# Layer 2's dense product by seven block products, with its sums in the last attention step, and another order of VectorE's work

## The chip, the cores and the metric

The kernel runs on one core of a Trainium2 chip. The time is the device time of one execution in microseconds (us). Nine executions of the kernel before lie between 1560.4 and 1579.48 us, with a median of 1569.6. One more was profiled. The names of the engines in the profile are PE (TensorE), PEld (its weight loads), DVE (VectorE), ACT (ScalarE), POOL (GpSimd) and SP (SyncE, which here issues DMAs only).

## The reference: four layers on 1024 tokens

The input `x` holds 8 sequences of 128 tokens with 512 features, in float32. Four layers add to it in turn, `x = x + ffn(cond(x))`. Layers 0, 1 and 3 are gated low-rank layers. Layer 2, which the change touches, is grouped attention over a paged cache followed by a dense layer with a small mixture:

```
q = rope(rmsnorm(x Wq));  k = rope(rmsnorm(x Wk));  v = x Wv        # 32 query heads, 8 key heads, D = 128
scores = q [k_cache[block_table], k]^T / sqrt(D), masked beyond cache_seqlens
o = softmax(scores) [v_cache[block_table], v];   y = o Wo             # y: 1024 x 512

H = y W^T + b                                                         # the dense product, 1024 x 512 x 512
z = y A                                                               # rank 32
w = weights of 8 experts, from H[anchor tokens, :8] and (z LiMEs^T)[anchor tokens]
x = x + H + ((z * (w LiMEs)) Bmat) * scaling
```

`w` needs only eight columns of H on every second token, and these are computed apart from H.

## The kernel before, in words

**Layout.** Tokens lie in 8 blocks of 128. `x` stays in SBUF turned: features on partitions, [128, 4 chunks, 1024 tokens]. Layer 2's attention output `y` is built with tokens on partitions, and each block is transposed by TensorE into `y2T`, which is laid out as `x` is.

**Attention.** `run` (line 1275) goes over 16 steps: 8 head groups (`qd`), and in each 4 pairs of blocks (`p`). Step `n` does the scores and exponentials of its first block (`weigh(n, 0)`, line 1122), the sums of the exponentials over the five key chunks (`added`, line 1144), the division and output block sums of the step before (`divided`, `outputs`), the projection of the step after (`project(n + 1)`, line 1000), the rotary terms (`rotate`, line 1041), the output projection of the step before (`leave(n - 1)`, line 1201), and then the second block's scores mixed with the first block's value products (`mix`, line 1176), the softmax sums by matmul (`summed`), their reciprocals (`inverted`) and the second block's value products. `project` and `leave` do a 2x2 block product with seven block products instead of eight (`seven`, line 952, Strassen's scheme in Winograd's form): sums of the blocks are made on VectorE beforehand, and partial results are added on VectorE between products that stay in the same PSUM banks. Their argument `at` names the places in `seven` where other engines' work is put into the order: "one", "six", "u1", "u2", "c22", "c11", "c12".

Keys and rotated queries are turned by VectorE in 32x32 squares into a buffer "kt", written to DRAM by four DMAs (`turn_cached`, line 1086, for the cached keys; `turn`, line 1102, for the new ones) and read back in the turned form (`fetch`, line 1113). Both use the one "kt" buffer. `gather` (line 899) reads cached keys and values by indirect DMAs that POOL issues.

**What sets the order.** Every instruction that goes through `kept` (line 855) is pinned behind the one traced before it on its engine. What does not go through it is placed by the framework's planner, which simulates the program. Before the change the functions of `ending` (line 1690) that deal with layer 2's dense part are mostly not pinned, and neither are the two loads of its weights.

**Layer 2's dense part.** `load_w2` and `load_aw` (lines 1748, 1752) load W and layer 3's A at step 14, into the buffers of the attention weights. `shifted` (line 1785) adds the bias to `x` with two POOL instructions of 128x2048. `turn` (line 1756) transposes a block of `y`; `low` and `anchors` (lines 1764, 1773) compute z and the routing columns from it, for blocks 0 to 3 at the end of step 14 and for 4 to 7 after the last step. `product(b)` (line 1792) does 16 matmuls of 128x128 by 128 columns for one block into a PSUM bank that stays open; `delta` (line 1879) adds the low-rank part into the same bank and VectorE adds the bank to `x` (line 1888, 128x512). `layer2` (line 2141) calls these, with `routing` (a chain of some twenty small VectorE instructions, line 1806) and `gains` (line 1855), and then prepares layer 3's weights on TensorE (`weights_turned`, `fold_scores`).

**Layer 3** already has a class `Seven` (line 1975) for block products of 256 columns: `begin` does the first product and copies it, `go_on` does the other six with three additions on VectorE between them. An open result is spread over two PSUM banks and two SBUF tiles; `last` (line 2124) adds these to `x`.

Of the kernel before, what the change touches and what calls it, by code (L numbers as in the profile page):

```python
# [17 lines left out]
P = 128  # L18
# [29 lines left out]
def forward(ctx: ExitStack, tc: tile.TileContext, a: dict, out: bass.AP):  # L48
# [615 lines left out]
    with psa:  # L664
# [73 lines left out]
        end.layer2(y2, bank, do=range(NB - 2, NB))  # L738
# [22 lines left out]
    with tc.If(redo > 0):  # L761
        sp.dma_start(x, kept)
        y2 = attention_any(tc, a, x, ident, lens, kvrow, part, ww, wop, ypool, eps, rows, chunks, mm)
        with ExitStack() as c3:
# [19 lines left out]
            end.layer2(y2, bank)  # L784
# [3 lines left out]
def attention(tc, a, x, ident, lens, kvrow, part, ww, wop, ypool, sums, rot, eps, psa, c2, chunks, mm):  # L788
# [412 lines left out]
    def leave(n, at={}):  # L1201
# [10 lines left out]

        def to_last(u):
            kept(pool.tensor_tensor(y(1, 1), u, y(1, 1), ALU.add))

        def to_middle(u):
            t = y2[:, 2 * p : 2 * p + 2, :].rearrange("p j d -> p (j d)")[:, HW : 3 * HW]
            t = t.rearrange("p (k d) -> p k d", k=2)
            kept(pool.tensor_tensor(t, t, u.unsqueeze(1).to_broadcast([P, 2, HW]), ALU.add))  # L1219
# [55 lines left out]
    def run(pool_, end_of, bank, keep):  # L1275
# [11 lines left out]
        rotate(1)()  # L1287
# [11 lines left out]
        for n, (qd, p) in enumerate(steps):  # L1299

            after = n + 1 if 0 < n < len(steps) - 1 else None
            weigh(n, 0)
            sums_of, outs = added(n, 0), iter(())
            next(sums_of)
            some(w_ops)()
            if n:
                divided(n - 1)
                outs = outputs(n - 1)
            every(sums_of)
            if after:  # L1310
# [7 lines left out]
                if n + 2 < len(steps):  # L1318
# [7 lines left out]
                    "u2": lambda: (keys_terms(), every(wo_ops)),  # L1326
                    "c22": lambda: (rotated(after), normed(after), turn(after)),
# [3 lines left out]
            elif n:  # L1331
                every(outs)
                leave(n - 1)
            else:
                read_cached = turn_cached(1)
                every(tokens(2))
                gather(2, "k")
            if n + 2 == len(steps):
                end.load_w2()
                end.load_aw()  # L1340
                end.shifted()
            mixed = mix(n, 0)
            weigh(n, 1, {2: (some(mixed),), 3: (some(mixed),), 4: (some(mixed, NC),)})
            if n == 0:
                fetch(1, read_cached)
            every(added(n, 1))
# [4 lines left out]
            inverted(n)  # L1351
            if n == 5:
                prepared = end.prepare(bank, lambda shape, name: wk.tile(shape, F32, tag="xs", name=name, bufs=1))
# [22 lines left out]
        end.product(0, "st", bank)  # L1376
        leave(n)
        return y2, end
# [311 lines left out]
def ending(  # L1690
# [25 lines left out]


    L3 = SimpleNamespace()
    Y2T = []
# [27 lines left out]

    def load_w2():
        W["2"] = tile_of_w2([P, DC, D], "WT2")
        sp.dma_start(W["2"], chunks(a["W2T"]))  # L1750

    def load_aw():
        W["a"] = tile_of_aw([P, DC, D], "AwT")
        sp.dma_start(W["a"], chunks(a["AwT"]))
# [30 lines left out]
    def shifted():  # L1785

        for g in range(TG):
            pool.tensor_tensor(
                x[:, :, half(g)], x[:, :, half(g)], bcol.unsqueeze(2).to_broadcast([P, DC, 512]), ALU.add
            )  # L1790

    def product(b, tag, bank):

        ps = bank(tag, [P, DC, P], f"h_{b}")
        for o in range(DC):
            for c in range(DC):
                mmq(
                    ps[:, o, :], W["2"][:, c, o * P : (o + 1) * P], Y2T[0][:, c, b * P : (b + 1) * P],
                    o == 0 and c == 0, False,
                )  # L1800
        H[b] = ps
# [77 lines left out]
    def delta(g):  # L1879

        zp, Bm = Z["zp"], L3.Bm
        for o in range(DC):
            for j in range(HB):
                mmq(H[g * HB + j][:, o, :], Bm[slot(j), o * P : (o + 1) * P], zp[slot(j), g, :], False, True)
        for j in range(HB):
            b = g * HB + j
            t = x[:, :, b * P : (b + 1) * P]
            dve.tensor_tensor(t, H[b], t, ALU.add)
# [60 lines left out]

    def left_sums(a11, a12, a21, a22, t, by):
        s1, s2, s3, s4 = (t[:, k] for k in range(4))
        for o, l, r, op in (
            (s1, a21, a22, ALU.add), (s2, s1, a11, ALU.subtract),
            (s3, a11, a21, ALU.subtract), (s4, a12, s2, ALU.subtract),
        ):
            by.tensor_tensor(o, l, r, op)
        return a11, a12, a22, s1, s2, s3, s4

    def right_sums(b11, b12, b21, b22, t):
        t1, t2, t3, t4 = (t[:, k] for k in range(4))
        for o, l, r in ((t1, b12, b11), (t2, b22, t1), (t3, b22, b12), (t4, b21, t2)):
            dve.tensor_tensor(o, l, r, ALU.subtract)
        return b11, b21, b22, t1, t2, t3, t4

    def left(t, k):

        return [t[:, 2 * j : 2 * j + 2, (2 * k + i) * P : (2 * k + i + 1) * P] for i in range(2) for j in range(2)]

    def right(t, g):

        return [t[:, 2 * i : 2 * i + 2, g * 512 + j * 256 : g * 512 + (j + 1) * 256] for i in range(2) for j in range(2)]

    class Seven:


        def __init__(self, name, bank, A, B):
            self.A, self.B = A, B
            self.even, self.odd = (bank("mm", [P, 2, 256], f"{name}_{i}") for i in range(2))  # L1980
            self.p1, self.u = (
                L3.w3.tile([P, 256], F32, tag=f"seven_{n}", name=f"{n}_{name}", bufs=2) for n in ("p", "u")
            )
            self.c = {(0, 0): (self.even[:, 0], None), (0, 1): (self.odd[:, 1], self.u),
# [288 lines left out]
```

## Time and profile before

| | |
|---|---|
| median of 9 executions | 1569.6 us |
| lowest, highest | 1560.4, 1579.48 us |
| the profiled execution | 1572.14 us |
| its span in the profile | 1570.3 us |
| mean granted TensorE clock | 0.993 |
| DMA | 169.92 MB, mean 108 GB/s |

By the timeline of TensorE the attention steps run from 332 to 1426 us, about 34 us for most of them. The end of layer 2, from the last value products to layer 3's first matmul, is the stretch from 1414 to 1470 us; layer 3 ends the program.

In a line of the timeline the first number is the start in us from the span's beginning, then the length, the engine, the line of the kernel, the operation, output and inputs, the shape, and the number of instructions in the row. Brackets hold the engine's idle time just before and what ended it. One float32 matmul is two MATMUL instructions here. A line of the waits gives engine, tile and line of the waiting instruction, what released it, the sum in us, how many times, and the longest. A line of the windows gives start and end of a stretch, its length, the busy time (and instructions) of PE, PEld, DVE, ACT and POOL, the granted clock, the DMA engines' busy share, and GB/s.

### The profile page before, as it was taken

The numbers are of one execution on the slowest core, as the hardware profiler recorded it, in microseconds if no ns is written. First come the engines' busy times: TensorE is split into PE (matmuls) and PEld (weight loads), VectorE is DVE, ScalarE is ACT, GpSimd is POOL, SyncE is SP. The second block draws the span as 40 slices with busy tenths as digits, with TensorE's granted clock in tenths as the row PEclk, the third lists the DMA queues.
The fourth block names the chain that finished last, engine by engine and source line by source line (L and its number), as shares of the span: only waits on it lengthen the run. The fifth ranks groups of instructions, "written<-read, shape, count | busy, mean of one in ns | idle before, by whom it ended". The sixth has DMA issues, their size and how long they took to land.

```text
span 1570.3 us, 19040 instructions
## 1 busy us (share of the span) xinstructions
PE 1523.2 (97%) x6127; PEld 952.5 (61%) x6127; DVE 1063.0 (68%) x2055; ACT 540.1 (34%) x1332; POOL 861.0 (55%) x874
## 2 busy tenths in 40 slices
PE   9999999989999999999999999999999999999998
PEld 7878786535555555555555555655555555558887
DVE  4666434477877777777777677777777878744375
ACT  1111110144444444444443434544444444310110
POOL 1331105285766777767677766767766777622220
PEclk9999999999999999999999999999999999999999
DMA  9111002144654444553454444345454435512001
GB/s 300 41 41 31 1 0 62 52 137 104 176 149 132 143 121 129 145 155 98 126 163 118 123 139 146 99 131 170 119 138 119 138 98 147 145 41 90 1 2 56
DMA packets 157837, 169.92 MB, mean 108 GB/s; under 512 B 54272, under 2 KB 129216, under 8 KB 157600
## 3 DMA queue, kind: packets, MB, share of 16 engines
q1 hardware_dynamic: 139296, 131.27, 29.8%
q0 software_dynamic: 17056, 36.49, 8.0%
q8 instruction: 51, 0.84, 0.2%
q10 hardware_dynamic: 1376, 0.85, 0.2%
q14 instruction: 58, 0.48, 0.1%
HBM read 113.89 MB, written 42.07 MB: 99 GB/s over the span
## 4 chain that ended last, share of the span: by engine, by line
PE 85%; DVE 8%; DMA 3%; issue 2%; POOL 1%; SPq 1%; ACT 0%; ACTq 0%; DVEq 0%; POOLq 0%
PE av L1181 17%; PE st L1130 17%; PE g L362 7%; PE q_six L966 7%; PE wo_two L966 5%; PE dn L362 5%; PE q_five L966 4%; PE q_one L966 4%; PE wo_six L966 3%; PE wo_one L966 3%; PE eo_l L53 2%; PE h L1710 2%; DVE os L925 2%; PE z L1710 2%; PE midp_l L53 1%
## 5 line engine op out<-in xcount | busy, mean ns | idle before, releaser
L909 POOL DMA_INDIRECT kn<-in_k_cache,kvrow_k x256 | 285.9, 1117 | 73.2 <-issue 69.2
L1181 PE MATMUL av<-pT,vals 128*128 128x512 f32 x640 | 300.4, 600 | 0.0
L909 POOL DMA_INDIRECT vals<-in_v_cache,kvrow_v x256 | 259.1, 1012 | 73.4 <-issue 62.9
L1134 ACT ACTIVATE pT<-st,hide 128x512 f32<-128x512 f32 x256 | 175.9, 687 | 333.7 <-PE st L1130 203.7
L1130 PE MATMUL st<-qT,kT 128*128 128x512 f32 x512 | 238.3, 598 | 1.7 <-DMA qT<-turned_new 1.7
L1055 POOL TENSOR_TENSOR vq<-q,txq 128x256 f32<-128x256 f32 x128 | 120.4, 967 | 185.7 <-DVE q L1015 110.0
L1181 PEld LDWEIGHTS av<-pT,vals 128*128 128x128 f32 x640 | 119.6, 191 | 145.0 <-issue 142.7
L1130 PEld LDWEIGHTS st<-qT,kT 128*128 128x128 f32 x512 | 98.0, 192 | 111.5 <-issue 108.4
L1150 DVE TENSOR_TENSOR part<-pT 128x512 f32<-128x512 f32 x128 | 88.3, 692 | 71.8 <-issue 44.0
L1166 DVE RECIPROCAL rr<-sum 128x256 f32<-128x256 f32 x32 | 56.2, 1757 | 58.2 <-PE sum L1159 50.7
L966 PE MATMUL q_one<-q,x 128*128 128x384 f32 x256 | 93.0, 486 | 0.0
L1039 ACT ACTIVATE sqq<-q 128x128 f32<-128x128 f32 x256 | 79.4, 310 | 25.7 <-DVE q L1015 18.8
L966 PEld LDWEIGHTS q_one<-q,x 128*128 128x128 f32 x256 | 48.5, 190 | 39.8 <-issue 14.4
L966 PE MATMUL q_six<-q_s,xs_all 128*128 128x384 f32 x192 | 69.8, 486 | 0.0
L1219 POOL TENSOR_TENSOR y<-y,uo 128x512 f32<-128x512 f32 x32 | 41.3, 1291 | 48.0 <-DVE y L1211 47.5
L966 PE MATMUL wo_one<-o,oT 128*128 128x256 f32 x256 | 65.7, 379 | 0.0
L1130 PE MATMUL st<-qT,kTn 128*128 128x512 f32 x128 | 65.4, 592 | 0.0
L1020 ACT COPY q<-q_one 128x256 f32<-128x256 f32 x32 | 11.9, 372 | 149.6 <-PE q_one L966 149.6
L966 PE MATMUL wo_two<-o_s,os 128*128 128x256 f32 x256 | 60.6, 380 | 2.4 <-DVE os L925 2.2
L966 PE MATMUL q_six<-q_s,x 128*128 128x384 f32 x128 | 48.9, 504 | 10.3 <-DVE vals L1015 10.3
L429 POOL TENSOR_TENSOR ws<-wu 128x256 f32<-128x256 f32 (+1 forms) x9 | 6.8, 756 | 94.2 <-DMA wu<-in_WuT 94.2
L1134 ACT ACTIVATE pT<-st,rs 128x512 f32<-128x512 f32 x64 | 44.0, 687 | 38.4 <-PE av L1181 19.6
(448 smaller groups left out, 2840.5 us busy)
## 6 DMA issues: line engine op xcount, KB each, us to landing
turned_new<-qkt SPq DMA_DIRECT2D x126, 160.0 KB
turned_cached<-kt SPq DMA_DIRECT2D x128, 128.0 KB
kT<-turned_cached SPq DMA_DIRECT2D x32, 512.0 KB
qT<-turned_new SPq DMA_DIRECT2D x32, 512.0 KB
R<-R SPq DMA_DIRECT2D x96, 128.0 KB
q<-in_WqT SPq DMA_DIRECT2D x8, 1024.0 KB
o<-in_WoT SPq DMA_DIRECT2D x8, 1024.0 KB
kn<-in_k_cache,kvrow_k POOLq DMA_INDIRECT x256
```

The source lines that it names most:

```text
L53: pe.matmul(o, lhsT, rhs, start=start, stop=stop)
L362: pe.matmul(o, lhsT, rhs, start=start, stop=stop, skip_group_check=True)
L909: kept(pool.indirect_dma_start(out=d[:, c, :], out_offset=None, in_=kc if what == "k" else vc, in_offset=bass.IndirectOffsetOnAxis(ap=kvro ...
L966: kept(pe.matmul(o, l[:, c, :], r[:, c, :], start=start and c == 0, stop=c == 1, skip_group_check=True))
L1039: kept(act.activation(sq, S[n][m][:, j, i, :], AF.Square, accum_out=S[n]["ssq"][:, j, col : col + 1]))
L1055: kept(pool.tensor_tensor(to, t[:, b, :, hi : hi + 64], wx[:, b, lo : lo + 64].unsqueeze(2).to_broadcast(list(to.shape)), ALU.mult,))
L1130: kept(pe.matmul(ps, s["kT"][:, c, 4 * j : 4 * j + 4, :] if c < 4 else s["kn"][:, j], s["qT"][:, :, REP * j : REP * (j + 1), :].rearrange( ...
L1134: kept(act.activation(pT[:, c, :, :].rearrange("p i t -> p (i t)"), ps, AF.Exp, **(dict(bias=hide[:, b, c : c + 1]) if c < 4 else dict(bia ...
L1150: kept(dve.tensor_tensor(o, l, r, ALU.add))
L1166: kept(dve.reciprocal(r, S[n]["sum"]))
L1181: kept(pe.matmul(ps, v[:, c, :], pT[:, c, :, :].rearrange("p i t -> p (i t)"), start=c == 0, stop=c == NC - 1, skip_group_check=True,))
L1710: return pe.matmul(o, lhsT, rhs, start=start, stop=stop, skip_group_check=True)
```

## The change

1. The dense product is done by four `Seven`s (two halves of the tokens `g`, two halves of the output features `k`) instead of eight calls of `product`: 56 matmuls of 256 columns for 128 of 128 columns. `Seven` is split in `begin`, `go_on` (three products) and `end` (three more), and `into_x` adds its results to `x`: three additions of an SBUF tile and four of a PSUM block, each 128x256, on VectorE.
2. `delta` gets banks of its own, and still adds 128x512 from each to `x`.
3. The block sums of W (eight VectorE instructions of 128x256, `product_weights`) and those of the first half of `y2T` (four of 128x512, `product_tokens(0)`) are placed in step 15 behind the first block's scores and ahead of `added(15, 0)`. Those of the second half come in `layer2`.
4. The `begin` and `go_on` of the first half come before `leave(15)`, the `end`s behind it: one before the last transposes, the other behind `low(1)` and `anchors(1)`, all pinned.
5. In step 15 `outputs(14)` goes ahead of the remaining sums of `added`, and `leave(14)` moves into the second block's scores, behind the third of them.
6. `leave(15)` has its last two additions on VectorE instead of POOL.
7. In `leave`'s "c22" slot the addition of the finished block now goes ahead of the weight sums and of the key's straight terms, which stood in "u2" ahead of it.
8. At the beginning `turn_cached(1)` moves from step 0 to before `turn(1)`; in step 0 `fetch(1)` and `gather(2, "k")` move behind the first two part sums of the second block, and `tokens(2)` behind the reciprocal.
9. `shifted` becomes four ACT instructions of 128x1024, in step 15 behind its last exponential; before, the planner placed its two POOL instructions in steps 13 and 14.
10. The two weight loads are pinned on SP, so they stand behind `fetch(15)` and ahead of the copies of R(14).

```diff
         def put(j, i):
             return lambda ps, u=None: kept(dve.tensor_tensor(y(j, i), ps, y(j, i), ALU.add))
+        by = dve if n + 1 == len(steps) else pool
         def to_last(u):
-            kept(pool.tensor_tensor(y(1, 1), u, y(1, 1), ALU.add))
+            kept(by.tensor_tensor(y(1, 1), u, y(1, 1), ALU.add))
...
-        rotate(1)()
+        keys_terms = rotate(1)
+        read_cached = turn_cached(1)
+        keys_terms()
         gather(1, "v")
         roots(1)
...
             weigh(n, 0)
+            if n and not after:
+                end.product_weights()
+                ts = [wk.tile([P, 2, 2, 256], F32, tag=t, name=f"ys_{t}", bufs=1) for t in ("q", "vq")]
+                end.product_tokens(0, *(t[:, k] for t in ts for k in range(2)))
             sums_of, outs = added(n, 0), iter(())
             next(sums_of)
             some(w_ops)()
             if n:
                 divided(n - 1)
                 outs = outputs(n - 1)
+                if not after:
+                    every(outs)
             every(sums_of)
...
-                    "u2": lambda: (keys_terms(), every(wo_ops)),
-                    "c22": lambda: (rotated(after), normed(after), turn(after)),
+                    "c22": lambda: (every(wo_ops), keys_terms(), rotated(after), normed(after), turn(after)),
                 })
                 fetch(after)
                 gather(after, "v")
-            elif n:
-                every(outs)
-                leave(n - 1)
-            else:
-                read_cached = turn_cached(1)
-                every(tokens(2))
-                gather(2, "k")
             if n + 2 == len(steps):
                 end.load_w2()
                 end.load_aw()
+            mixed = mix(n, 0)
+            left = (lambda: leave(n - 1),) if n and not after else ()
+            weigh(n, 1, {2: (some(mixed), *left), 3: (some(mixed),), 4: (some(mixed, NC),)})
+            if left:
                 end.shifted()
-            mixed = mix(n, 0)
-            weigh(n, 1, {2: (some(mixed),), 3: (some(mixed),), 4: (some(mixed, NC),)})
+            sums_of = added(n, 1)
             if n == 0:
+                some(sums_of, 2)()
                 fetch(1, read_cached)
-            every(added(n, 1))
+                gather(2, "k")
+            every(sums_of)
...
             inverted(n)
+            if n == 0:
+                every(tokens(2))
...
         divided(n)
         every(outputs(n))
-        end.product(0, "st", bank)
+        t = wk.tile([P, 4, 256], F32, tag="xs", name="h_sums", bufs=1)
+        for k in range(2):
+            end.product(0, k, bank, ("st", "av" if k else "st"), (t[:, 2 * k], t[:, 2 * k + 1]))
         leave(n)
+        end.added_product(0, 0)
+        for j in range(2):
+            end.turn(y2, NB - 2 + j, bank)
+        end.low(1, bank)
+        end.anchors(1, bank)
+        end.added_product(0, 1)
         return y2, end
...
+        def begin(self):
+            self.into(self.even[:, 0], self.A[0], self.B[0], True)
+            pinned(act.copy(self.p1, self.even[:, 0]))
+        def go_on(self):
...
+            self.into(odd[:, 1], s1, t1, True)
+            self.into(odd[:, 0], s2, t2)
+            pinned(dve.tensor_tensor(u, odd[:, 0], p1, ALU.add))
+            pinned(dve.tensor_tensor(p1, odd[:, 1], p1, ALU.add))
+            self.into(even[:, 1], s3, t3)
+            pinned(dve.tensor_tensor(p1, even[:, 1], p1, ALU.add))
+        def end(self):
...
+            self.into(odd[:, 1], s4, b22)
+            self.into(even[:, 0], a12, b21)
+            self.into(even[:, 1], a22, t4)
...
+    def load(n, tile, src):
+        t = tile([P, DC * D + 8 * P], "w_" + n)
...
+        kept(sp.dma_start(W[n], chunks(src)))
...
     def shifted():
-        for g in range(TG):
-            pool.tensor_tensor(
-                x[:, :, half(g)], x[:, :, half(g)], bcol.unsqueeze(2).to_broadcast([P, DC, 512]), ALU.add
-            )
+        for c in range(DC):
+            kept(act.activation(x[:, c, :], x[:, c, :], AF.Identity, bias=bcol[:, c : c + 1]))
+    def product(g, k, bank, tags, sums=None):
+        f = H[g, k] = Seven(f"h_{g}_{k}", bank, S["w2"][k], S["y2", g], tags, sums)
+        f.begin()
+        f.go_on()
+    def added_product(g, k):
+        f = H[g, k]
+        f.end()
+        into_x(f, g, k)
+    def into_x(f, g, k, then=lambda o, tok: None):
...
+        for (i, j), (_, more) in reversed(f.c.items()):
+            if more is not None:
+                t = block(i, j)[0]
+                pinned(dve.tensor_tensor(t, t, more, ALU.add))
+        for ij in ((1, 1), (0, 1), (0, 0), (1, 0)):
+            t, o, tok = block(*ij)
+            pinned(dve.tensor_tensor(t, f.c[ij][0], t, ALU.add))
+            then(o, tok)
...
-    def layer2(y2, bank, held=lambda: None, do=range(NB)):
...
+    def layer2(y2, bank, do=()):
+        order[0] = lambda i: i
...
+        product_tokens(1, *spare(0))
+        product(1, 0, bank, ("st", "st"))
+        added_product(1, 0)
         routing()
         gains(bank)
-        product(HB, "av", bank)
-        delta(0)
-        for b in range(HB + 1, NB):
-            product(b, "mm", bank)
+        product(1, 1, bank, ("mm", "mm"))
+        added_product(1, 1)
+        delta(0, bank, ("av", "av", "st", "st"))
...
         weights_turned(free)
-        delta(1)
+        delta(1, bank, ("av", "av", "mm", "mm"))
         fold_scores(free)
```

`pinned` is `kept` until `layer2` sets `order[0]`, and nothing from there on, so the second half of the product is placed by the planner.

## The prediction, on record before the run

> **What bounds the kernel now.** I read the page's engine shares first, then its chain of work that ended last, then the list of TensorE's own waits, and last the timelines around each wait.
>
> ```profile
> PE 1523.2 (97%) x6127; PEld 952.5 (61%) x6127; DVE 1063.0 (68%) x2055; ACT 540.1 (34%) x1332; POOL 861.0 (55%) x874
> ```
> ```profile
> PE 85%; DVE 8%; DMA 3%; issue 2%; POOL 1%; SPq 1%; ACT 0%; ACTq 0%; DVEq 0%; POOLq 0%
> ```
>
> TensorE is busy for 1523 of 1570 us and carries 85% of the chain. So only two things shorten the kernel: less matmul time, and fewer of TensorE's 47 idle us. The waits of TensorE (sum, times, longest):
>
> ```profile
> PE q_six L966 <- DVE vals L1015: 10.3, 19, 0.8
> ...
> PE sum L1159 <- issue: 3.4, 1, 3.4
> PE wo_two L966 <- DVE uo L981: 3.2, 2, 1.8
> PE wo_six L966 <- DVE y L1211: 2.3, 8, 0.5
> ...
> PE wo_two L966 <- DVE os L925: 2.2, 1, 2.2
> ...
> PE y2T L1761 <- POOL y L1219: 0.7, 1, 0.7
> ```
>
> The largest, 10.3 us, lies in `project`, whose "u2" slot the diff leaves alone: it stays. The other five can be laid beside an edit each.
>
> **The product.** These are two stretches of TensorE's timeline, the old product and a row of matmuls of the new shape (two instructions are one fp32 matmul):
>
> ```profile
> 1447.54 10.98 PE L1710 MATMUL h<-y2T,WT 128*128 128x128 f32 x96
> ```
> ```profile
> 1398.11 1.03 PE L966 MATMUL wo_one<-o,oT 128*128 128x256 f32 x4
> 1398.97 1.03 PE L966 MATMUL wo_two<-o,os 128*128 128x256 f32 x4
> ```
>
> From start to start (the next row, W3p, is at 1458.37) 48 matmuls of 128 columns take 10.83 us, 0.226 each; the 128 of `product` take 28.9 us by that. Two of 256 columns take 0.86 us. Four `Seven`s of 14 such matmuls are 56, 24.1 us. `delta` keeps its 32 short ones. Saved: **4.8 us**. For this the old product must have no idle under it, and the windows say so: TensorE is busy 12.5 of 12.5 us and 12.0 of 12.0 from 1434 to 1458.5.
>
> **The first step (n = 0).** Here `sum` waits 3.4 us. The chain behind it on VectorE: turn(1)'s transpose ends at 338.48, and turn_cached(1), which shares the single buffer "kt", stands still until the four writes of the first have landed:
>
> ```profile
> 343.50 1.30 DVE L1091 STREAM_TRANSPOSE kt<-kn 128x512 f32<-128x512 f32 x2 [2.32 <-DMA turned_new<-qkt]
> ```
> ```profile
> 349.02 0.43 PE L1159 MATMUL sum<-part,ones 128*32 128x128 f32 x8 [3.41 <-issue]
> 349.38 6.25 PE L1181 MATMUL av<-pT,vals 128*128 128x512 f32 x10
> ```
>
> Two transposes (1.3 us) and tokens(2) (1.4 us) stand ahead of the second block's part sums. The change takes both out, the first to before turn(1), the second behind the reciprocal. The buffer wait comes along: turn_cached(1) can start when its keys have landed (last gather issued by POOL until 330.5, plus an estimated 2.5, so 333.0 to 333.7), its four writes take the 5.0 us that the other four took (338.48 to 343.50), and turn(1) starts at 338.7 instead of 336.97. Then 1.5 us of transpose and eight part sums at 0.69 end near 345.7; TensorE wants them at 345.55. The stall of 3.4 becomes 0 to 1.5. SP's queue: the four cached writes go first, then turn(1)'s, end near 342.2, and qT is read 2.8 us later, as in step 2 (381.48 to 384.26), at 345.0, with kT half a us behind. TensorE will want them at 355.47-3.4-1.7 = 350.4; in step 0 the first scores came 4.8 us after qT's issue (327.35 to 332.15). So a new wait of 0 to 3.4, nearer nothing; I take 0.7. POOL's gather(2,"k") now follows fetch(1); it fed nothing before 366.9. Net **-2.7 us**.
>
> The `av` row shows a second loss: ten instructions take 6.25 us, elsewhere 4.56. The clock was down after the stall:
>
> ```profile
> 345.00:350.00 5.00, 1.59 (x18) 0.71 (x18) 4.28 (x9) 0.00 (x0) 4.09 (x4) 0.95 0.72 179
> 350.00:355.00 5.00, 5.00 (x9) 2.01 (x8) 2.41 (x5) 0.00 (x0) 3.78 (x5) 0.71 1.04 294
> ```
>
> The eighth number is the granted clock. A dip of 0.05+0.29 of 5 us costs **1.7 us** and goes with the stall. [...]
>
> **The bias shift.** In steps 13 and 14 `shifted` runs on POOL and VectorE stands behind it:
>
> ```profile
> 1285.74 3.60 POOL L1788 TENSOR_TENSOR x<-x,bcol 128x2048 f32<-128x2048 f32 x1
> ```
> ```profile
> 1285.74 4.67 DVE L1060 TENSOR_TENSOR r<-q,tsq 128x1024 f32<-128x1024 f32 x1
> ```
>
> Elsewhere that VectorE line takes 1.77 us. `wo_two` waits 1.8 and 1.5 us behind it: **-3.2 us**. The four ACT instructions of 128x1024 that replace it have no row; the exponential of 128x512 takes 0.69, so 2.4 to 5.5 us. They follow the last exponential of step 15, where ACT is idle 7.8 us (1407.6 to 1415.4): nothing. Without that cover `y2T` of block 5 would be late by what sticks out.
>
> **VectorE's order in `leave`.** The add of the block that frees `six` now goes ahead of keys_terms (0.55) and the remaining weight sums (0.94): the 2.3 us of wo_six go, and what they hid behind is done in the same time; **-2.2**, between 0 and 2.3. rotated, which is next, starts no later, the sum of VectorE's work being the same.
>
> **The last step.** VectorE is idle 1379.6 to 1389.7 but for 0.5 us. Twelve new sums go there: eight of 128x256 (0.39 each, by the `os` rows) and four of 128x512 (0.69): 5.9 us. They wait for W2, whose load is now pinned on SP behind fetch(15); before, it was issued at 1354.72. qT should go at about 1373 (2.8 us after the writes that end at 1370.24), W2 at 1375, AwT and R's copies behind it. The window 1380 to 1385 moved 215 GB/s; 1 MB at that is 5 us, so W2 lands at 1380 to 1385, and R, behind 2 MB, by 1388. Sums end at 1386 to 1391; behind them on VectorE wait the part sums, `divided` (1.3) and `outputs`, which now goes ahead of the other part sums; the second `os` is 2.8 us after, 1389 to 1394. `leave`(14) has meanwhile been moved behind three scores and one `av` (3.4 us) and wants it at 1396. So the 2.2 us wait goes: **-2.2**; if W2 came 5 us later it would be back. to_middle and to_last on VectorE (0.69+0.42 for POOL's 1.98) let the block turn earlier, and end(0,0) lies over it: **-0.7**.
>
> **The tail.** The new product gives VectorE ten short operations per `Seven`. From the end of leave(15) to layer 3's first matmul its work is then: 28 adds of `into_x` and six of `go_on` at 0.41 (13.9), four token sums (2.8), `delta` as now (5.0), routing with its copies (5.3), a turn (0.7), checks and layer 3's weight sums as now (5.4): 33 us, in a stretch that lasts 42 now (1428 to 1470). low(1) and anchors(1) must now come before end(0,1), on two fresh copies. No row shows this arrangement. Bounds: 0, and 9 us if VectorE goes in program order and routing starts behind two `into_x`, token sums and `go_on`. I take **+1.7**, near the lower end, since after 1458.5 TensorE has W3p, kwp and fkp that need no VectorE.
>
> Sum: -4.8 -2.7 -1.7 -3.2 -2.2 -2.2 -0.7 +1.7 = -15.8. The profiled execution took 1572.1 (span 1570.3), giving 1556.3; it is 2.5 above the median of 1569.6, so against the median 1553.8: **1554**. A measurement tells about 0.5%, 7.8 us, from no change.
>
> **Rivals.** *The tail gives the product back* (0.20): VectorE is the bound after 1428. For it: 33 us of work in a stretch of 42 less what is saved, and POOL's sixteen weight sums of 0.7 us run there too; the row of 4.67 us says that such a POOL operation can stop VectorE. Against it: W3p and fkp fill TensorE. It costs 8 of the 9 us bound above: -15.8+8 = -7.8, 1562. [...]
>
> *The new order does nothing* (0.09): what its words say of VectorE's order would not be so. Step 0 waits for kT as long as it waited for `sum` (2.7 back), the dip stays (1.7), W2 comes late enough to bring the 2.2 back, and low(1) gets a dip as low(0) has one with the same small matmuls (2.8 us in the eight `st` instructions at 1385.16, 6.37 for 3.60). -15.8+9.4 = -6.4: 1563.
>
> *Slower* (0.05): VectorE's tail decides alone. The other edits give 15.8-4.8+1.7 = 12.7 us, so the stretch of 42 must last over 54.7. VectorE's 33 us, 11.5 of being stopped by sixteen POOL sums, 11.1 of routing from hd to zp (1434.3 to 1445.4) as waiting with nothing beside it, and two dips of 3.4 make 62.4: 7.7 over, 1577. It decides only if all of POOL's sums fall on VectorE's and nothing covers the routing; that the planner now lays 3.5 us of checks and other work into that stretch speaks against it.
>
> **Numbers.** Forecast 0.66. Best end: all of the stalls (no 0.7, no 1.7) and one dip of 3.4 less in the tail, 1548; two us less for the median's own spread. Upper end: past the first two rivals, with three us for the spread. 1546 to 1566. Faster by over 0.5% (below 1561.8): the forecast and 0.12 of the first rival, 0.78; within: 0.17; slower 0.05.
>
> **What would show it.** TensorE's waits without `sum` at 3.4, without `uo` and `os`, and with wo_six under 0.3; L1060 near 1.77 in all steps; matmuls of h at 256 columns, 112 instructions in 24 us; clock near 1 from 345 to 355. Wrong: waits of h on DVE in the tail over 3 us, a wait of `st` on kT near 350, or one of `wo_two` on `os` in step 15.

## The result, and the profile after

The kernel after takes 1557.69 us (median of 18 executions, 1553.28 to 1566.53); the kernel before, run beside it, 1568.71 us (55 executions). The ratio is 0.994, with a 95% interval of 0.9925 to 0.9955: by the medians 11.0 us less. The profiled execution of after took 1561.0 us, with a span of 1559.2 and a mean granted clock of 0.989 (before 1572.14, 1570.3 and 0.993).

A correction first, which every later number needs: eight head groups of four pairs of blocks are 32 steps, n = 0 to 31, and not 16. What the text ahead, the prediction and the expectations call step 15 is step 31, the last; steps 1 to 14 are steps 1 to 30, and what is said of step 14 holds for step 30. The two instructions of `shifted`, which they put into steps 13 and 14, lie in steps 28 and 30: in the profile of before they start at 1285.7 and 1356.9 us, and these steps at 1271.5 and 1342.1. The durations and the working do not depend on it.

The engines' shares of after:

```profile
PE 1517.9 (97%) x5983; PEld 948.5 (61%) x5983; DVE 1066.3 (68%) x2113; ACT 545.7 (35%) x1340; POOL 834.2 (54%) x870
```

TensorE has 144 instructions and 5.3 us less than before, and is still busy for 97%. Its largest waits:

```profile
PE st L1130 <- ACT pT L1134: 6.4, 1, 6.4
PE pT L1975 <- DVE p L1967: 5.3, 1, 5.3
PE q_six L966 <- DVE vals L1015: 4.8, 8, 0.8
...
PE h L1727 <- DVE zgT L1754: 1.4, 1, 1.4
```

(`st` are the scores, and `pT` is the transposed form of the routing weights `p`, which end a chain of small VectorE instructions.) All five waits that the prediction laid beside an edit are gone. But the two largest are new, and q_six, which was to stay at 10.3, is at 4.8. So the sum cannot have come about as written. I cut both spans at the same events on TensorE's timeline: the first scores (`st`) of step 0, the first `q_one` after them, the first scores of step 31, the end of the last value products (`av`), layer 3's first matmul (`midp_l`), and the end. The right-hand columns are the second pair of profiles, made later (e5_before_again and e6_after_timed below, both on one chip):

| stretch | predicted | first pair, before | after | difference | second pair, before | after | difference |
|---|---|---|---|---|---|---|---|
| up to the first scores | 0 | 332.2 | 331.3 | -0.9 | 333.6 | 329.5 | -4.2 |
| step 0 | -4.4 | 27.6 | 30.5 | +2.9 | 27.7 | 22.7 | -5.0 |
| steps 1 to 30 | -5.4 | 1025.4 | 1006.0 | -19.4 | 1003.7 | 995.4 | -8.2 |
| step 31 | -2.2 | 29.4 | 25.9 | -3.4 | 26.7 | 24.5 | -2.3 |
| tail | -3.8 | 55.8 | 63.6 | +7.7 | 55.7 | 63.3 | +7.7 |
| layer 3 | 0 | 100.0 | 101.9 | +1.9 | 100.1 | 100.3 | +0.2 |

The tail is the same in both pairs: it does not win 3.8 us, it loses 7.7. (Two further kernels with the old product, e1_order and e2_step0 below, have a tail of 53.6 us; against them the loss is 10.) In step 0 and in steps 1 to 30 the two pairs do not agree, and what differs there is not the kernel.

My theory at this point (A): the edits in the attention steps bring far more than predicted, and the product's gain is more than given back in the tail. Rivals: the product brings its 4.8 us and something else made the tail longer (B); and, for step 0, the moved gather causes a new wait, or that wait comes from the execution.

### The profile page after: what moved, and what is told of

Read it like the earlier page. It is cut to its first block, busy times and chain, and to the rows that moved or that the text cites. A ratio compares the mean times of both kernels' runs of the same rounds, so it can differ in the third digit from the quotient of the medians.

```text
span 1559.2 us, 18842 instructions
## 1 busy us (share of the span) xinstructions
PE 1517.9 (97%) x5983; PEld 948.5 (61%) x5983; DVE 1066.3 (68%) x2113; ACT 545.7 (35%) x1340; POOL 834.2 (54%) x870
## 4 chain that ended last, share of the span: by engine, by line
PE 87%; DVE 6%; DMA 3%; issue 2%; another core or an unknown queue 1%; ACT 0%; POOL 0%; SPq 0%; ACTq 0%; DVEq 0%; POOLq 0%
PE st L1130 17%; PE av L1181 17%; PE g L362 7%; PE q_six L966 7%; PE wo_two L966 5%; PE dn L362 5%; PE q_five L966 4%; PE q_one L966 4%; PE wo_six L966 3%; PE wo_one L966 3%; PE eo_l L53 2%; PE z L1727 2%; PE h L1727 2%; PE midp_l L53 1%; PE o L1727 1%
## 5 line engine op out<-in xcount | busy, mean ns | idle before, releaser
L909 POOL DMA_INDIRECT kn<-in_k_cache,kvrow_k x256 | 274.3, 1071 | 73.3 <-issue 70.3
L1020 ACT COPY q<-q_one 128x256 f32<-128x256 f32 x32 | 11.9, 372 | 145.4 <-PE q_one L966 145.4
L362 PE MATMUL g<-xs,ws 128*128 128x256 f32 (+1 forms) x240 | 56.9, 388 | 1.4 <-POOL ws L429 1.4
L1134 ACT ACTIVATE pT<-st,rs 128x512 f32<-128x512 f32 x64 | 44.0, 687 | 39.2 <-PE av L1181 28.8
L966 PEld LDWEIGHTS wo_one<-o,oT 128*128 128x128 f32 x256 | 48.6, 190 | 13.4 <-PE st L1130 0.2
```

Of the source, the lines that this page charges most:

```text
L362: pe.matmul(o, lhsT, rhs, start=start, stop=stop, skip_group_check=True)
L909: kept(pool.indirect_dma_start(out=d[:, c, :], out_offset=None, in_=kc if what == "k" else vc, in_offset=bass.IndirectOffsetOnAxis(ap=kvro ...
L966: kept(pe.matmul(o, l[:, c, :], r[:, c, :], start=start and c == 0, stop=c == 1, skip_group_check=True))
L1134: kept(act.activation(pT[:, c, :, :].rearrange("p i t -> p (i t)"), ps, AF.Exp, **(dict(bias=hide[:, b, c : c + 1]) if c < 4 else dict(bia ...
```

## The experiments

The runs were made in three groups of four, each group on one chip with its own executions of the kernel before (medians 1547.74, 1548.59 and 1561.31 us; 1568.71 in the comparison above). So only ratios and differences within a group are compared.

### Each edit of the attention steps alone, and all three

e1_order is the kernel before with edit 7:

```diff
-                    "u2": lambda: (keys_terms(), every(wo_ops)),
-                    "c22": lambda: (rotated(after), normed(after), turn(after)),
+                    "c22": lambda: (every(wo_ops), keys_terms(), rotated(after), normed(after), turn(after)),
```

> The kernel before with edit 7 alone: in leave's c22 slot the addition of the finished block ahead of the weight sums and of the key's straight terms. Theory A (VectorE's order made the gain of steps 1 to 14, 19.4 us between the two profiles, of which 3.4 are shifted's): 14 to 16 us less than before, ratio 0.990 to 0.991, and project's q_six and q_five waits fall from 10.3 and 3.6 us to about 4 and 1. Rival B (the prediction's term, the wo_six waits alone): 2.2 us less, ratio 0.9986, q_six still near 10 us. Under both the step 0 stall of sum (3.4 us) and the two uo waits stay.

e2_step0 is the kernel before with edit 8 (the lines of the diff above for `rotate(1)`, `fetch(1)`, `gather(2, "k")` and `tokens(2)`).

> The kernel before with edit 8 alone: turn_cached(1), fetch(1), gather(2,k) and tokens(2) moved at the beginning. Prediction's term: 4.4 us less than before (sum stall and clock dip gone, 0.7 of new wait), ratio 0.997. Rival, by the profile after: the stall of sum goes, but a wait of st on ACT of some 6 us with a dip of 6.8 us at half clock comes instead, 2 to 3 us more than before, ratio 1.0015 to 1.002. If that wait was chance and not the change's doing, it is not in this profile and the first holds. Steps 1 to 14 are as before under both.

e3_789 has edits 7, 8 and 9, with the old product.

> The kernel before with edits 7, 8 and 9 (VectorE's order, step 0, shifted on ACT), with the old product of 128 matmuls and the old last step. Theory A (the seven-product form and what is laid around it in the tail cost more than they bring: the profile after stands 3.4 us better in step 15 but 7.7 us worse in the tail and 1.9 worse in layer 3): 15 to 18 us less than before, ratio 0.989, so some 5 us better than the whole change. Rival (the product form brings its 4.8 us and the last step 2.9): 3 to 5 us less than before, worse than the whole change by 6 us or more, ratio 0.997.

e4_after_again is the whole change once more.

> The whole change once more, for its profile. If the 6.4 us wait of st on ACT in step 0 belongs to the change, it is there again at about the same place (within 2 us), and so is the half clock from 354 to 361; if it was chance, the row of st at 358 has an idle time under 1 us. The wait of pT on p in the tail (5.3 us) is there again under both.

Measured: e1_order 0.9977 [0.9957, 0.9997], e2_step0 0.9978 [0.9964, 0.9991], e3_789 0.9916 [0.9897, 0.9935], that is 3.6, 3.4 and 13.0 us less than before; e4_after_again once, 1541.33 us, 6.4 below the median of before. e3_789 without the product is 6.1 us faster than this one execution of the whole change, as theory A expects.

In TensorE's waits of e2_step0, which lacks edit 7, stands

```profile
PE st L1130 <- DMA qT<-turned_new: 4.8, 3, 1.8
PE wo_six L966 <- DVE y L1211: 3.8, 9, 0.8
```

and in those of e1_order, which has it,

```profile
PE sum L1159 <- DVE part L1150: 6.7, 3, 3.6
PE st L1130 <- DMA qT<-turned_new: 3.3, 3, 1.8
```

wo_six is gone, as predicted, and q_six on vals is in neither list, with or without edit 7. So both numbers that I had expected of theory A for e1_order were wrong: edit 7 is not worth 14 to 16 us, and it is not what took q_six from 10.3 to 4.8. From e2_step0 to e1_order the stretch of steps 1 to 30 goes from 1005.1 to 999.4, by 5.6 us. 3.8 of it are wo_six; the steps in which weight sums are made take 33.0 us instead of 33.6. Of the rest 2.0 lie in step 25, where a wait of 1.6 us for qT goes. That step takes 33.1 us in e4_after_again and 34.4 in e6_after_timed, which are the same kernel, so these 2.0 us need not be the edit's.

Step 0 takes 27.6 us in e1_order and 22.3 in e2_step0: 5.3 us. In e4_after_again it takes 22.3 as well, without any wait of st on ACT. So that wait isn't the change's doing alone.

### The kernel before and after again, on another chip

> The kernel before once more, for its profile beside the others of this call. If VectorE's late starts behind TensorE (the reciprocal of the softmax sums begins 0.3 to 2.7 us after the last sums matmul ends, in the first two profiles) belong to the kernel, they are here again, with q_six waits near 10 us; if they belong to the chip or the execution, the reciprocal begins 0.07 us after in all steps, the q_six waits are under 1 us, and the steps 1 to 14 take 1005 to 1012 us instead of 1025.

> The whole change, timed beside the two kernels with a mended tail. Both theories: 6 to 11 us less than before, ratio 0.993 to 0.996; in the profile the tail (from the end of the last value product to layer 3's first matmul) takes 63.5 us, with a wait of 5.2 us of pT on p.

Measured: e5_before_again 1549.39 us, e6_after_timed 0.9936 [0.9915, 0.9956] (9.9 us less). The two are the second pair of the table. In the kernel before, q_six on vals is not in TensorE's list any more; its larger waits in the attention steps are

```profile
PE sum L1159 <- DVE part L1150: 4.8, 2, 3.5
PE wo_six L966 <- DVE y L1211: 4.0, 10, 0.8
PE st L1130 <- DMA qT<-turned_new: 3.0, 2, 1.7
...
PE wo_two L966 <- DVE os L925: 2.3, 1, 2.3
```

What differs between the first pair and this one can be read from two rows of step 1, in the same kernel. The timeline of after, first profile (the softmax sums on TensorE, and the reciprocal on VectorE that needs only them):

```profile
386.03 0.64 PE L1159 MATMUL sum<-part,ones 128*32 128x128 f32 x16
...
389.59 1.76 DVE L1166 RECIPROCAL rr<-sum 128x256 f32<-128x256 f32 x1 [4.43 <-PE av L1181]
```

The same in e6_after_timed:

```profile
376.35 0.64 PE L1159 MATMUL sum<-part,ones 128*32 128x128 f32 x16
...
377.06 1.76 DVE L1166 RECIPROCAL rr<-sum 128x256 f32<-128x256 f32 x1 [1.58 <-PE sum L1159]
```

In e6_after_timed VectorE starts 0.07 us after the end of the last sums matmul, in the first profile 2.9 us after it, though it was idle. In e1 to e8 the reciprocals start 0.05 to 0.3 us after it in all 32 steps. In the first pair, and in e9 to e12, it is 0.2 to 0.8 us in most steps and up to 3.5 in some, and back to 0.07 in the last step, in which no keys are gathered any more. TensorE's own pace is the same in both (an undisturbed step takes 33.01 us). So in these two groups of executions VectorE and ACT start late behind TensorE (ACT's exponentials of step 1's first block begin in after at 357.73 us, 5.7 us behind the end of the scores at 352.04), and q_six, q_five and the st of step 0 wait for it. The reciprocals that start 1.0 us or more late are all ones at which POOL is still issuing gathers when the sums end; in e1 to e8 gathers stand there as well and delay nothing.

The traces differ in one more thing, which bears on the names in the lists of waits: that of the first before holds 8027 records of DMA landings, that of e5_before_again 17760. The same stall of step 0 stands under `issue` in the one and under `part` in the other.

In e1 to e8 and in e9 to e12 all kernels of a chip agree in this, so it goes with the chip, or with the time at which the group ran, and not with the kernel. Why is open.

### The bias shift alone, and the product alone

e9_shift is the kernel before with edit 9; e10_product has all edits but 7, 8 and 9.

```diff
-        for g in range(TG):
-            pool.tensor_tensor(
-                x[:, :, half(g)], x[:, :, half(g)], bcol.unsqueeze(2).to_broadcast([P, DC, 512]), ALU.add
-            )
+        for c in range(DC):
+            kept(act.activation(x[:, c, :], x[:, c, :], AF.Identity, bias=bcol[:, c : c + 1]))
```

> The kernel before with edit 9 alone: the bias shift as four ACT instructions in step 15 in place of two POOL instructions in steps 13 and 14. Prediction's term: 3.2 us less than before, ratio 0.998, the VectorE line L1060 at 1.77 us or less in all steps and no wait of wo_two on uo or of sum on part behind it. If the rest of the difference between e1_order, e2_step0 and e3_789 is this edit's, 4 to 5 us less, ratio 0.997.

> The kernel before with edits 1 to 6 and 10, that is the seven-product form with its sums in step 15 and the tail around it, without the moves of edits 7, 8 and 9. Theory A: 4 to 8 us more than before, ratio 1.003 to 1.005, since the tail takes 63 us instead of 55.7 and the last step gains 2.3 to 2.7. Prediction's terms (product 4.8, last step 2.9, tail back 1.7): 6 us less, ratio 0.996.

Measured: e9_shift 0.9976 [0.9962, 0.9991], 3.7 us less; e10_product 1.0036 [1.0021, 1.0051], 5.6 us **more** than before. The product form by itself, with what is laid around it, makes this kernel slower: theory A, within the 4 to 8 us expected. The tail's +7.7 and step 31's -2.3 in the second pair make 5.4.

The two profiles lie on one chip and differ in steps 1 to 30 by edit 9, and by when the weight loads go out in step 30: 1010.3 us in e9_shift, 1015.3 in e10_product. The timeline of e10_product, where the shift still runs on POOL, at step 30:

```profile
1345.33 3.60 POOL L1883 TENSOR_TENSOR x<-x,bcol 128x2048 f32<-128x2048 f32 x1
...
1345.64 4.37 DVE L1060 TENSOR_TENSOR r<-q,tsq 128x1024 f32<-128x1024 f32 x1
```

and that of e9_shift at the same place:

```profile
1343.67 1.77 DVE L1060 TENSOR_TENSOR r<-q,tsq 128x1024 f32<-128x1024 f32 x1
```

The VectorE instruction, begun 0.31 us behind POOL's, takes 2.6 us more. In step 28 of e10_product VectorE's begins first, at 1273.37 against 1273.51: there it takes 1.27 us, and POOL's takes 4.59 where it took 3.60. On a chip without late starts the price of edit 9 can be read more cleanly: from e1_order to e3_789 steps 1 to 27 agree within 0.2 us each, and steps 28 to 30 take 5.1 us less.

This group also prices the first pair. Steps 1 to 30 take 1015.3 us in e10_product, 1004.0 in e11_route_only and 1003.3 in e12_fold_early, which have edits 7, 8 and 9: 11 to 12 us for the edits on a chip with late starts. The first pair shows 19.4. Between the first before and e10_product, whose work in these steps is the same, lie 10 us. So some 8 us of the 19.4 belong to the executions that happened to be profiled. Step 0 with edit 8 takes 30.7 us in e12_fold_early, with the same wait on ACT as in after (5.2 us; there 6.4), but 24.4 in e11_route_only (1.6), against 27.6 and 28.0 without it. The reciprocal of step 0 starts 0.07 us after its sums in e9_shift and e10_product and 0.9 and 3.5 us after them in e11_route_only and e12_fold_early. So on this chip the late start in step 0, and the wait on ACT behind it, come with edit 8; on the two chips of e1 to e8 edit 8 brings neither. Which of its four moves does it (the moved gather is one) was not tried.

### The tail: what it waits for

The tail of after in the first profile, the waits ahead of `pT`:

```profile
1431.12 1.02 PE L1975 MATMUL pT<-ident,p 128*8 128x128 f32 x4 [5.26 <-DVE p L1967]
1432.81 0.65 PE L1727 MATMUL pmix<-pTs,Li 8*32 8x64 f32 x16 [0.66 <-ACT pTs L1977]
```

`p` is the end of the routing chain on VectorE, which begins when `hd` is there. In after:

```profile
1415.45 0.19 DVE L1876 TENSOR_TENSOR hd<-hd,b 128x32 f32<-128x32 f32 x1 [0.74 <-PE hd L53]
...
1430.61 0.46 DVE L1967 TENSOR_TENSOR p<-p,s 128x32 f32<-128x32 f32 x1
```

In before:

```profile
1434.30 0.19 DVE L1779 TENSOR_TENSOR hd<-hd,b 128x32 f32<-128x32 f32 x1 [0.75 <-PE hd L53]
...
1440.51 0.19 DVE L1852 TENSOR_TENSOR p<-p,s 128x32 f32<-128x32 f32 x1
```

15.6 us from hd's start to p's end, where it was 6.4: between the links of the chain stand token sums, `into_x` and layer 3's weight sums. Before, TensorE had 80 instructions of `h` to do meanwhile. This is the timeline of e5_before_again:

```profile
1411.32 9.18 PE L1710 MATMUL h<-y2T,WT 128*128 128x128 f32 x80
1420.33 0.60 PE L1860 MATMUL pT<-ident,p 128*8 128x128 f32 x4
```

VectorE's work in the tail went from 57 instructions and 21.7 us to 103 and 38.7. The windows of the tail say so, of e5_before_again

```profile
1391.72:1447.37 55.65, 54.42 (x505) 51.10 (x503) 21.68 (x57) 6.29 (x14) 14.01 (x20) 0.96 0.21 62
```

and of e6_after_timed:

```profile
1372.04:1435.37 63.33, 54.94 (x360) 46.14 (x359) 38.74 (x103) 7.88 (x18) 12.11 (x18) 0.89 0.19 54
```

The clock, third from the end, is at 0.89 there, and TensorE idles 8.4 us where it was 1.2.

Three kernels take this apart. e7_weights_early is the whole change with one line moved:

```diff
         added_product(1, 0)
+        weights_turned(free)
         routing()
         gains(bank)
...
-        weights_turned(free)
```

> The whole change with layer 3's weight transposes (weights_turned) traced ahead of routing and gains, so that the planner can lay their 3.8 us of TensorE's time into the wait for p. Theory A (the product's gain is lost because TensorE has nothing left while VectorE's routing chain runs, and the half clock follows the idle stretch): the wait of pT falls from 5.2 to about 1.5 us, one dip of half clock goes, 4 to 7 us less than the whole change, ratio to before lower by 0.0025 to 0.0045. Rival B (VectorE's work is the bound of the tail, so what TensorE does meanwhile is indifferent): the wait moves to zp or to the products behind it, within 1.5 us of the whole change.

e11_route_only moves another:

```diff
+        routing()
         product_tokens(1, *spare(0))
         product(1, 0, bank, ("st", "st"))
         added_product(1, 0)
-        routing()
```

> The whole change with routing traced ahead of the token sums and the third product, weights_turned left where it is. If the end of the routing chain on VectorE is what the tail waits for, this alone gives what e8_route_first gave: 4 to 6 us less than the whole change, ratio to before 0.990 to 0.991, pT waiting under 2.5 us. If TensorE's lack of work counts as much, half of that or less, ratio 0.992 to 0.994, pT waiting 3 us or more.

e8_route_first moves both.

> As e7_weights_early, and routing traced ahead of the token sums and of the third product as well, so that its chain does not stand in the queue behind x's additions. Theory A: p comes 5 us or more earlier than in the whole change, no wait of pT over 1 us, the tail takes 53 to 57 us instead of 63.5, 6 to 10 us less than the whole change. Rival B: x's additions and the token sums come later by what routing comes earlier, the third product waits for its sums 2 us or more longer, and the tail gains under 3 us.

| kernel | ratio to before | tail | wait of pT | p after hd's start |
|---|---|---|---|---|
| e6_after_timed | 0.9936 [0.9915, 0.9956] | 63.3 | 5.0 | 15.4 |
| e7_weights_early | 0.9945 [0.9923, 0.9966] | 63.5 | 3.7 | 16.9 |
| e11_route_only | 0.9931 [0.9906, 0.9956] | 61.2 | 2.6 | 13.5 |
| e8_route_first | 0.9900 [0.9879, 0.9920] | 57.1 | none | 12.3 |

e7_weights_early went by rival B in its time: TensorE does its transposes (1403.24 to 1406.2) in the wait, `p` comes no earlier, and the end is where it was. The idle TensorE is filled for nothing here, since the chain behind the wait is what ends last. e11_route_only, which is on another chip (e10_product has a tail of 63.6 us there), gives 2.5 us of tail, by its ratio the second of its two cases, though pT waits 2.6 us and not 3. Both moves together give 6.3 us of tail, and 4.8 us by the medians (1538.09 to 1533.33), between what A and B expected. In e8_route_first:

```profile
1406.40 0.60 PE L2047 MATMUL wq3p<-ident,Wq 128*16 128x128 f32 x4
1406.83 0.60 PE L1975 MATMUL pT<-ident,p 128*8 128x128 f32 x4
1408.26 0.43 PE L1727 MATMUL pmix<-pTs,Li 8*32 8x64 f32 x16 [0.83 <-ACT pTs L1977]
```

p is there 3.1 us sooner, pT stands right behind the other transposes, and it takes 0.60 us where it took 1.02. In e6_after_timed a clock of 0.50 is granted for 6.83 us from 1407.68, 3.5 us into the idle stretch that began at 1404.17; in e8_route_first it isn't: the 0.93 of its tail comes from half clock at fkp alone, from 1420.43 on. TensorE works for 4.64 of these 6.83 us, and half of that, by the clock of 0.50, with the 3.1 us makes 5.4 of the 6.3 gained.

e8_route_first is faster than the whole change: its slowest execution takes 1534.51 us, the fastest of e6_after_timed 1535.83. But e3_789, with the old product, has nearly the same ratio (0.9916, interval 0.9897 to 0.9935); the two were not run on one chip, so it is not shown that the new product with a mended tail gains anything over the old one.

### The half clock at fkp

All kernels with the new product also have 10.2 us or more of half clock at `fkp`, the 64-column products for layer 3. Of those with the old product before, e3_789, e5_before_again and e9_shift have 6.83 there, and e1_order and e2_step0 none. The last experiment takes fkp away from the short products of `delta`: e12_fold_early is e8_route_first with one more line moved.

```diff
         weights_turned(free)
+        fold_scores(free)
         gains(bank)
...
         delta(1, bank, ("av", "av", "mm", "mm"))
-        fold_scores(free)
```

> As e8_route_first, with the products of narrow tiles for layer 3 (kwp, fkp, gkp: 64 columns) traced ahead of gains as well, so that they stand before the last dense product and not in one row with the 64 short products of delta. If half clock comes from a row of narrow products (d, kwp, fkp, gkp in one stretch of 10 us), the dip of 10.2 us at fkp falls to 6.8 us or less, the tail takes 52 to 55 us and the kernel 2 to 5 us less than e8_route_first, ratio 0.987 to 0.989. If the half clock comes from the idle stretches, it changes by under 1 us.

Measured: 0.9896 [0.9867, 0.9926], not to be told from e8_route_first; the tail takes 58.9 us. The dip isn't shorter; it moved along with fkp. The timeline of e8_route_first has

```profile
1420.08 6.79 PE L53 MATMUL fkp<-kw,W 128*128 128x64 f32 x32 [0.52 <-ACT kw L2030]
```

and e12_fold_early

```profile
1430.04 6.17 PE L53 MATMUL fkp<-kw,W 128*128 128x64 f32 x32
```

The windows of e12_fold_early at this place, the first being the 3.41 us ahead of the half clock:

```profile
1427.45:1430.86 3.41, 3.06 (x37) 2.56 (x36) 1.22 (x2) 1.46 (x4) 3.41 (x6) 1.00 0.00 0
1430.86:1441.10 10.24, 10.24 (x42) 9.61 (x42) 1.96 (x4) 0.96 (x3) 6.30 (x9) 0.50 0.01 2
```

TensorE is busy for 3.06 of 3.41 us in the window before, with pT, kwp, pmix, two instructions of h and the first of fkp, and the clock is halved all the same. So both expectations fell: this dip follows no idle stretch (the longest in that window is 0.35 us), and it isn't the neighbourhood of delta. What stays is that the half clock begins 0.3 to 2.3 us into fkp's row in e5, e6, e8 and e12, wherever that row stands. But the row alone does not bring it: e1_order runs the same instructions at full clock.

```profile
1431.43 3.79 PE L53 MATMUL fkp<-kw,W 128*128 128x64 f32 x32 [0.46 <-ACT kw L1913]
```

What decides between the two was not taken apart.

## Why the prediction was right, and where not

The time came out at 1557.7, inside the range and 3.7 us above the forecast; against the two profiles the sum is -11.1 where -15.8 was written. That it lies so near is in part luck. Edits 7 to 9 were put at -9.8 and brought -13.0 (e3_789); edits 1 to 6 and 10 were put at -6.0 and brought +5.6 (e10_product). The first error made up for part of the second, whose sign was wrong. Point by point:

- **The product's own matmuls, -4.8: right.** In e4_after_again the 32 instructions of the first two products start at 1373.64 and what follows them at 1380.55: 0.432 us a matmul, 24.2 for 56. In e5_before_again 40 old ones take 9.01 (1411.32 to 1420.33), 28.8 for 128. Saved: 4.6 to 4.7.
- **The tail, +1.7: the step that failed.** The stretch went from 55.7 to 63.3 us, so with the 4.7 of the product and the 0.7 of y it gave back 13.1, more than the upper bound of 9. I named the price of that bound correctly (the routing chain standing behind into_x, token sums and go_on: 9.2 us measured), and then took a value near zero "since TensorE has W3p, kwp and fkp that need no VectorE". They are traced behind gains, the planner put them behind pT, and nothing was left for the wait. By e7_weights_early they would not have helped: what ends last is VectorE's chain. The second pair adds up so: -4.7 product, +5.0 wait of pT, +2.1 waits of h, +0.7 pmix, -0.75 the old wait of y2T, +3.8 half clock (11.9 us of it fall on TensorE's work, against 4.3 before, counted at half by the granted clock of 0.50): +6.1 of the 7.7; the other 1.6 I could not put down to rows. The sign I had named for it, waits of h on VectorE over 3 us, did not show (2.1): the wait fell on pT.
- **"The tail gives the product back" (0.20)** was thus the true mechanism, with a larger price than its 8.
- **Step 0, -2.7 and -1.7: right in mechanism and size** where VectorE and ACT start on time: -5.3 (e1_order to e2_step0) and -5.0 (second pair). The stall of sum is gone, scores do not wait for kT or qT, and the clock stays at 1. In the timing edit 8 alone brings 3.4 us (interval 1.4 to 5.6). A gather's landing, put at 2.5 us by an estimate that no row of before shows, takes 3.0 in the median in e5_before_again. On a chip with late starts the term lies between -3 and +3, because ACT's exponentials begin late (5.7 us in after) and the fourth scores matmul of step 1's first block, which the table counts to step 0, waits for its PSUM buffer. No row of before gave a hint of that wait; e9 to e12 show that it comes with edit 8 there.
- **The clock dip behind the stall: right.** In before, e1, e5, e9 and e10, which have the stall, half clock for 3.41 us follows; in e2, e3 and e6 there is neither. In before the half clock runs from 349.53 to 352.94; of the 3.41 us ahead of it (346.1 to 349.5) 2.9 are the stall and 0.5 work. How short a stall would still bring it was not tried.
- **The bias shift, -3.2: mis-sized.** It measured -5.1 in steps 28 to 30 where VectorE starts on time (e1_order to e3_789) and -5.0 on the other chip (1015.3 to 1010.3). The timing of e9_shift gave -3.7, with an interval of 1.4 to 5.9 us that holds 3.2 as well as 5. The sum had counted the two waits of wo_two, and not what else stood behind VectorE: in e1_order it is sum that waits for part, 3.1 us in steps 28 and 30, and in e3_789 it doesn't.
- **VectorE's order, -2.2: mis-sized, by the profiles above its bound.** 3.6 us in the timing (interval 0.5 to 6.7), and 5.6 in the profiles of one chip, of which 2.0 lie in step 25 and need not be its own. The wo_six waits themselves are 3.8 to 4.0 us where VectorE starts on time (e2_step0, e5_before_again), not 2.3.
- **"q_six stays": wrong, but not by the change.** It is not there at all in e1 to e8, with or without edit 7, and 4 to 5 us in e9 to e12, again with or without it. The wait belongs to the late starts, and the first before had most of it.
- **Step 31, -2.2: right** (-2.3; -2.7 from e3_789 to e4_after_again), and with it the y on VectorE: no wait of y2T on POOL is left.

## What to carry to other kernels

When a change takes matmuls out of a stretch, ask what those matmuls were covering: here 9 us of the old product lay over a chain of twenty small VectorE instructions, and the new form put its own sums between the links of that chain. Price a block-product form by the serial chain of the engine that makes its sums, not by the sum of its work; and where one bound of a term is "in program order", look up the trace order before taking a value near the other bound. And profile the kernel before twice before arguing from its waits: a wait of 10 us that the next execution does not have is no term of a sum.

## What the runs showed of the hardware

- In two groups of executions an idle VectorE began 0.2 to 3.5 us after the matmul it waited for in nearly all steps, 1.0 us or more only where POOL was still issuing gathers; in the others 0.05 to 0.3 us after it. The kernel before took 1568.7 and 1561.3 us in the former, 1547.7 and 1548.6 in the latter, with the same instructions and the same 33.01 us for an undisturbed step.
- Half the clock was granted for 6.8 to 13.7 us at `fkp` in twelve of the fourteen traces, and in the 3.41 us ahead of it TensorE was busy for 2.3 to 3.1 us. In e8_route_first its 32 instructions took 6.79 us, nearly all of it in half clock; in e3_789, with half clock for the last 1.9 us, 4.65; in e1_order and e2_step0, without any, 3.79.
- Begun 0.31 us behind a POOL addition of 128x2048, a VectorE instruction of 128x1024 (L1060) took 4.37 us (e10_product); without that addition it took 1.77 (e9_shift). Where VectorE's began 0.14 us ahead of it, POOL's took 4.59 us instead of 3.60, and VectorE's 1.27 (e10_product).
